# Local attention on one core: the scores of the first two query blocks joined in one matmul, and a new order of a step's pieces

## The chip, the cores and the metric

The kernel runs on one core of one Trainium2 chip. A core has a matrix engine (TensorE, PE in the profile, with its weight loads shown apart as PEld), a vector engine (VectorE, DVE), a scalar engine (ScalarE, ACT), a general engine (GpSimd, POOL) and a queue engine (SyncE, SP) that issues DMAs. Each has its own stream of instructions and works through it in order; semaphores tie the streams together. The metric is the device time of one execution in microseconds.

## The reference, cut to what matters

The whole kernel computes four residual stages on `x` of 16 sequences, 128 tokens, 128 features: causal attention, six layers of local attention with feed-forward behind a geometric warp, gated linear attention, and expert layers. The change touches the six layers of local attention alone. Each has 16 heads of 64, and queries in four blocks of 32 that see their own block and the one before:

```python
def local_attention(q, k, v):
    b, h, n, d = q.shape
    w = WINDOW                      # 32
    nw = n // w                     # 4 blocks of 32 queries
    ...
    bk2, bv2 = (look(bk), look(bv)) # keys of the block before and of the block itself
    ...
    mask = (it < jb) | (it > jb + w) | (jb == -1)
    sim = jnp.einsum('bhwie,bhwje->bhwij', bq, bk2) * QK_SCALE
    sim = jnp.where(mask, -jnp.finfo(sim.dtype).max, sim)
    attn = jax.nn.softmax(sim, -1)
    out = jnp.einsum('bhwij,bhwje->bhwie', attn, bv2)
    ...
for i in range(DEPTH):              # 6
    x = attn_layer(shift_tokens(x), Wqkv[i], q_scale[i], k_scale[i], Wo[i]) + x
    x = ffn_layer(shift_tokens(x), ln_g[i], ...) + x
```

Block 0 has no block before it. The kernel lets it look at keys 0 to 63, as block 1 does, and the mask (the tile `band`) hides the keys of block 1 from it.

## The kernel before, in words

The kernel keeps all 16 sequences on the chip. A front stage does the first attention and the warp, a local stage the six layers (96 units: one unit is one sequence in one layer), and a tail the rest. In the trace scores() of the local stage runs from 467 us to 2110 us.

A unit's work is cut into **pieces**, one method call each:

- project (four matmuls of 128x512, queries and keys), square and cossin (ACT and DVE read the result), sum_squares, lengths, rotate, normalize_queries and normalize_keys: rotary embedding and lengths, on DVE, ACT and POOL
- transpose and keep_transpose: rotated queries and keys turned to `qkT0`, `qkT1`, through TensorE (L854) and ACT
- values, keep_values, shift: values, and four DMAs on SP's queue that place the neighbour block's values in `vx`
- scores (L882), mask, maxima, exponentials, normalize: the attention weights
- turn, keep_turn, weigh (L947), keep_weighed, out, add: weights times values, and the output projection
- the feed-forward of a group of four sequences: mean, center, square, variance, root, spread (two DMAs, through memory and back), scale, up, gelu, gate, down, add

Four units go through together in a pass of `STEP`, a list of pieces written out by hand. `p0` to `p3` are the projection pieces of the four units of the pass, `t0` to `t3` the attention pieces of the units two behind, `o0` to `o3` the weighing pieces of the units three behind; `f` is the feed-forward one group behind, `e`, `g` and `h` that two groups behind. `run_layers` runs STEP once for each group of four (a shorter list FIRST for the first). The pieces issue their instructions in the list's order on TensorE, DVE, ACT and POOL under a manual schedule: each engine does its own pieces in just this order, and waits where an operand isn't there. PSUM holds two score tiles (ring `s`) and four single banks (ring `g`).

scores() of a unit makes 16 heads' scores of 128 queries by 64 keys. Heads are taken in pairs: one head's 64 features lie in partitions 0 to 63 (`LO`), the other's in 64 to 127 (`HI`). For each pair, each half and each block of 32 queries there is one matmul with 32 columns of queries as weights and 64 columns of keys moving, 64 matmuls in all. In the built program each is declared as a tile of 64 rows by 32 columns of the array, and the places (two row halves, four column groups) make eight such tiles. weigh() has 48 matmuls, all declared as 64x64 tiles; the other matmuls of a step are declared as 128x128. An fp32 matmul appears in the trace as two passes, each with a weight load.

Of the kernel before, what the change touches and what calls it, by code (L numbers as in the profile page):

```python
# [314 lines left out]
class FirstUnit:  # L315
# [19 lines left out]
    def scores(self, half):  # L335

        sc = self.sc[half] = self.fr.ps("w")
        cols = slice((self.b % 2) * P, (self.b % 2) * P + P)
        T = self.halves[half].T
        for j in range(4):  # L340
            pr = 4 * half + j
            for k, rows in enumerate((LO, HI)):
                self.nc.tensor.matmul(
                    sc[:, k * 512 + j * P : k * 512 + j * P + P],
                    T[0][rows, pr, cols], T[1][rows, pr, cols], start=True, stop=True,
                )
# [417 lines left out]
class Unit:  # L764
# [111 lines left out]
    def scores(self):  # L876
        sc = self.sc = self.lo.ps("s")
        for pr in range(8):
            for k, rows in enumerate((LO, HI)):
                for i in range(4):  # L880
                    w = 32 * max(i - 1, 0)
                    self.nc.tensor.matmul(  # L882
                        sc[32 * i : 32 * i + 32, 512 * k + 64 * pr : 512 * k + 64 * pr + 64],
                        self.T[0][rows, pr, 32 * i : 32 * i + 32],
                        self.T[1][rows, pr, w : w + 64], start=True, stop=True,
                    )

# [189 lines left out]


STEP = """
p0.project(0,0) p0.project(0,1) p0.cossin(0,0) p0.cossin(0,1) p0.square(0,0) p0.project(1,0)  # L1080
t0.transpose(1,0) p0.square(1,0) p0.square(0,1) p0.project(1,1) p0.square(1,1) t0.values(0)
t0.keep_transpose(1,0) t0.keep_values(0) p0.cossin(1,0) t0.transpose(0,0) p0.rotate(0)
p0.cossin(1,1) t0.transpose(1,1) t0.transpose(0,1) t0.keep_transpose(0,0) t0.keep_transpose(1,1)
t0.keep_transpose(0,1) p0.sum_squares(0) o0.turn(0) e.variance() o0.keep_turn(0)
t1.transpose(1,0) e.root() t0.scores() t1.transpose(1,1) t1.keep_transpose(1,0)
p0.sum_squares(1) t1.keep_transpose(1,1) o0.turn(1) t0.mask() o0.keep_turn(1) p0.lengths()
t1.transpose(0,0) t1.keep_transpose(0,0) p1.project(0,0) p0.rotate(1) p0.normalize_queries()
t1.transpose(0,1) o0.weigh() p1.square(0,0) t0.maxima() t1.keep_transpose(0,1) t1.scores()
t0.exponentials(0) p1.cossin(0,0) p1.project(0,1) o0.keep_weighed(0) p1.cossin(0,1)
p1.project(1,0) o0.keep_weighed(1) t0.values(1) p1.square(0,1) e.spread() t0.keep_values(1)  # L1090
t2.transpose(0,0) t2.keep_transpose(0,0) p1.cossin(1,0) e.scale() t1.mask() p1.square(1,0)
o0.out() o0.add() p0.normalize_keys() p1.rotate(0) t0.normalize(0) t0.exponentials(1)
p1.project(1,1) t1.values(0) t1.keep_values(0) p1.cossin(1,1) t0.shift() g.up(2) p1.square(1,1)
g.gelu(2) g.up(1) g.gelu(1) g.gate(2) t2.transpose(1,0) g.gate(1) t2.transpose(0,1)
t2.keep_transpose(1,0) t2.transpose(1,1) p1.sum_squares(0) g.up(0) t2.keep_transpose(0,1)
t2.keep_transpose(1,1) o1.turn(0) t0.normalize(1) t1.maxima() g.gelu(0) o1.turn(1) p1.rotate(1)
g.gate(0) o1.keep_turn(0) p2.project(1,0) t1.exponentials(0) t1.values(1) o1.keep_turn(1)
p2.project(0,0) h.down() p1.sum_squares(1) p2.square(1,0) t1.keep_values(1) p1.lengths()
p1.normalize_queries() p2.cossin(0,0) p2.cossin(1,0) t1.normalize(0) p1.normalize_keys()
p2.project(0,1) h.add() p2.project(1,1) p2.cossin(0,1) p2.square(0,0) o1.weigh() t2.scores()  # L1100
t1.exponentials(1) p2.square(0,1) t3.transpose(0,0) p2.cossin(1,1) o1.keep_weighed(0)
p2.square(1,1) t2.mask() t3.transpose(0,1) t1.shift() t1.normalize(1) o1.keep_weighed(1)
t2.maxima() t3.keep_transpose(0,0) t3.transpose(1,0) t3.keep_transpose(0,1) t2.values(0)
t3.keep_transpose(1,0) t2.keep_values(0) p2.rotate(0) t3.transpose(1,1) o2.turn(0)
t3.keep_transpose(1,1) o2.turn(1) o2.keep_turn(0) o2.keep_turn(1) t3.scores() p2.sum_squares(1)
t3.mask() o2.weigh() p2.rotate(1) t2.exponentials(0) o2.keep_weighed(0) t2.values(1) o1.out()
p3.project(1,0) p2.sum_squares(0) o2.keep_weighed(1) t2.normalize(0) t2.keep_values(1)
t2.exponentials(1) p3.project(0,0) t3.maxima() o1.add() p3.square(0,0) t3.values(0) p2.lengths()
p3.cossin(1,0) p3.square(1,0) o2.out() t2.normalize(1) t2.shift() p3.cossin(0,0) o3.turn(0)
t3.keep_values(0) p2.normalize_queries() o3.turn(1) o2.add() p3.project(0,1) t3.exponentials(0)  # L1110
p2.normalize_keys() o3.keep_turn(0) o3.keep_turn(1) p3.cossin(0,1) p3.project(1,1) o3.weigh()
p3.square(1,1) p3.square(0,1) f.mean() p3.cossin(1,1) p3.rotate(0) p3.sum_squares(0)
o3.keep_weighed(0) o3.keep_weighed(1) t3.exponentials(1) t3.values(1) o3.out() p3.sum_squares(1)
t3.keep_values(1) p3.rotate(1) p3.lengths() f.center() t3.normalize(0) o3.add() t3.shift()
f.square() t3.normalize(1) p3.normalize_keys() p3.normalize_queries()
""".split()


# [896 lines left out]
```

## Time and profile before

| what | value |
|---|---|
| median of 3 runs | 2503.51 us (2493.62 to 2518.77) |
| the profiled execution | 2485.3 us, its span 2483.5 us |
| granted clock of TensorE, mean | 0.975 |
| PE, DVE, ACT, POOL busy, share of the span | 91%, 73%, 68%, 60% |
| PE matmul records, weight load records | 32244, 32244 |
| scores(), L882: matmul passes, busy | 12288, 158.8 us |
| weigh(), L947: matmul passes | 9216 |
| local stage (440 to 2120 us): PE busy | 1522.1 of 1680 us |

The page of a profile describes one execution on the chip. "Busy" is the time in which at least one instruction of an engine runs; tiles of the array that work side by side count once, so 12,288 passes of 0.226 us each make 158.8 us. Records of matmuls overlap, and their ends are modelled: what tells how fast TensorE goes is the distance from start to start. Idle time is listed with what ended it; "issue" means that the engine waited for nothing that the profile shows.

### The profile page before, as it was taken

The numbers are of one execution on the slowest core, as the hardware profiler recorded it, in microseconds if no ns is written. First come the engines' busy times: TensorE is split into PE (matmuls) and PEld (weight loads), VectorE is DVE, ScalarE is ACT, GpSimd is POOL, SyncE is SP. The second block draws the span as 40 slices with busy tenths as digits, with TensorE's granted clock in tenths as the row PEclk, the third lists the DMA queues.
The fourth block names the chain that finished last, engine by engine and source line by source line (L and its number), as shares of the span: only waits on it lengthen the run. The fifth ranks groups of instructions, "written<-read, shape, count | busy, mean of one in ns | idle before, by whom it ended". The sixth has DMA issues, their size and how long they took to land. (4 is left out here: it accounts for less than half of the span.)

```text
span 2483.5 us, 77001 instructions
## 1 busy us (share of the span) xinstructions
PE 2249.8 (91%) x32244; PEld 1540.3 (62%) x32244; DVE 1803.6 (73%) x2481; ACT 1695.4 (68%) x5814; POOL 1482.2 (60%) x1242
## 2 busy tenths in 40 slices
PE   7999998789899979998989999999899999789998
PEld 5676765466556656665656666666556666456766
DVE  6999998777677777777777778777677777454545
ACT  5888888577677757777777777777677777344422
POOL 3777776676566666666666776666666665243210
PEclk9999999999999989999999999999999999899999
DMA  3111114111111111211112111211111111212220
GB/s 111 31 30 32 28 31 112 35 36 36 40 57 52 36 39 37 66 44 32 44 44 67 39 44 37 70 39 40 30 37 37 38 34 41 60 51 69 72 73 26
DMA packets 120034, 116.67 MB, mean 47 GB/s; under 512 B 62914, under 2 KB 81928, under 8 KB 118920
## 3 DMA queue, kind: packets, MB, share of 16 engines
q1 hardware_dynamic: 108712, 87.62, 13.0%
q0 software_dynamic: 9216, 22.03, 2.9%
q8 instruction: 254, 4.16, 0.7%
q10 hardware_dynamic: 1760, 2.10, 0.3%
q14 instruction: 92, 0.75, 0.1%
HBM read 54.77 MB, written 6.60 MB: 25 GB/s over the span
## 5 line engine op out<-in xcount | busy, mean ns | idle before, releaser
L820 POOL TENSOR_TENSOR rot<-t 128x512 f32<-128x512 f32 x384 | 492.7, 1312 | 120.9 <-DVE t L794 120.8
L794 DVE TENSOR_TENSOR t<-g,tab 128x1024 f32<-128x1024 f32 x372 | 449.2, 1222 | 154.5 <-PE g L781 134.2
L907 ACT ACTIVATE pe<-s,nm 128x64 f32<-128x64 f32 x1536 | 460.5, 340 | 1.3 <-DVE nm L896 1.0
L916 POOL TENSOR_TENSOR pe<-pe,den 128x512 f32<-128x512 f32 x192 | 199.7, 1046 | 391.5 <-DVE den L915 317.6
L831 POOL TENSOR_TENSOR rot<-rot,r 128x1024 f32<-128x1024 f32 x192 | 363.1, 1909 | 52.3 <-ACT r L813 52.3
L781 PE MATMUL g<-wqkv,xs 128*128 128x512 f32 x744 | 377.8, 621 | 1.7 <-ACT sq L786 1.0
L907 ACT ACTIVATION_READ_ACCUMULATOR pe<-s,nm 128x1 f32 x1536 | 357.8, 233 | 0.0
L786 ACT ACTIVATE sq<-g 128x512 f32<-128x512 f32 x372 | 220.4, 600 | 182.4 <-DVE t L794 126.9
L859 ACT COPY qkT<-g 128x512 f32<-128x512 f32 x384 | 213.5, 592 | 122.8 <-PE g L854 122.5
L854 PEld LDWEIGHTS g<-ident,rot 128*128 128x128 f32 x1536 | 180.6, 145 | 105.2 <-issue 69.8
L882 PE MATMUL s<-qkT,qkT 64*32 64x64 f32 x12288 | 158.8, 226 | 85.0 <-issue 85.0
L804 DVE TENSOR_REDUCE ss<-sq 128x16 f32<-128x1024 f32 x192 | 229.8, 1208 | 0.0
L854 PE MATMUL g<-ident,rot 128*128 128x128 f32 x1536 | 220.1, 281 | 10.7 <-ACT ge L1049 6.6
L963 PEld LDWEIGHTS g<-oT,wo 128*128 128x128 f32 x1536 | 188.5, 195 | 39.1 <-issue 24.9
L839 PE MATMUL g<-wqkv,xs 128*128 128x512 f32 x384 | 208.2, 625 | 2.3 <-ACT qkT L859 2.2
L882 PEld LDWEIGHTS s<-qkT,qkT 64*32 64x32 f32 x12288 | 133.6, 106 | 105.6 <-issue 103.7
L963 PE MATMUL g<-oT,wo 128*128 128x128 f32 x1536 | 191.8, 279 | 2.4 <-ACT oT L955 2.4
L781 PEld LDWEIGHTS g<-wqkv,xs 128*128 128x128 f32 x744 | 131.0, 196 | 100.9 <-issue 69.4
L890 DVE TENSOR_TENSOR s<-s,band 128x1024 f32<-128x1024 f32 x96 | 117.9, 1228 | 87.4 <-PE s L882 87.2
L947 PE MATMUL g<-pT,vx 64*64 64x32 f32 (+1 forms) x6144 | 161.6, 218 | 19.5 <-issue 19.4
L450 POOL DMA_INDIRECT box<-fr_image,idx x128 | 157.0, 1227 | 33.6 <-issue 30.9
L947 PE MATMUL g<-pT,v 64*64 64x64 f32 (+1 forms) x3072 | 162.7, 228 | 14.0 <-issue 13.5
(345 smaller groups left out, 4540.9 us busy)
## 6 DMA issues: line engine op xcount, KB each, us to landing
vx<-v SPq DMA_DIRECT2D x384, 128.0 KB
wqkv<-in_lo_wqkv_dram SPq DMA_DIRECT2D x6, 1536.0 KB
roots<-lo_roots SPq DMA_DIRECT2D x23, 256.0 KB
fr_image<-xres SPq DMA_DIRECT2D x32, 104.0 KB
wo<-in_lo_wo_dram SPq DMA_DIRECT2D x6, 512.0 KB
box<-fr_image,idx POOLq DMA_INDIRECT x128
fr_moved<-out SPq DMA_DIRECT2D x16, 128.0 KB
w<-in_lo_w_dram SPq DMA_DIRECT2D x6, 341.0 KB
```

Source lines behind the costliest of these rows:

```text
L781: self.nc.tensor.matmul(pq, self.xT, self.w.qkv[:, at : at + 512], start=True, stop=True)
L786: self.nc.scalar.activation(self.bank["sq", k][:, c * 512 : c * 512 + 512], self.bank["q", k, c], AF.Square)
L794: self.nc.vector.tensor_tensor(self.t[k][:, :, 8 * c : 8 * c + 8, :], heads(self.bank["q", k, c]).unsqueeze(1).to_broadcast([P, 2, 8, 64]) ...
L804: self.nc.vector.tensor_reduce(self.ss[:, 16 * k : 16 * k + 16], heads(self.bank["sq", k]), AX.X, ALU.add)
L820: self.nc.gpsimd.tensor_tensor(self.rot[k][:, :, at], t[:, 0, :, at], t[:, 1, :, other], ALU.add)
L831: self.nc.gpsimd.tensor_tensor(self.rot[k], self.rot[k], self.r[:, 16 * k : 16 * k + 16].unsqueeze(2).to_broadcast([P, 16, 64]), ALU.mult,)
L854: self.nc.tensor.transpose(pt[:, j * P : j * P + P], flat[:, at : at + P], self.s.ident)
L859: self.nc.scalar.copy(self.T[k][:, 4 * c : 4 * c + 4, :].rearrange("p c t -> p (c t)"), self.bank["T", k, c],)
L882: self.nc.tensor.matmul(sc[32 * i : 32 * i + 32, 512 * k + 64 * pr : 512 * k + 64 * pr + 64], self.T[0][rows, pr, 32 * i : 32 * i + 32], s ...
L907: self.nc.scalar.activation(self.pe[half][:, n, :], heads(self.sc)[:, at, :], AF.Exp, bias=self.nm[:, at : at + 1], accum_out=self.den[:, ...
L947: self.nc.tensor.matmul(po[half][(LO, HI)[k ^ half], j * P + q0 : j * P + q0 + n], v, self.pT[half][rows, j, q0 : q0 + n], start=True, sto ...
L963: self.nc.tensor.matmul(self.pout[:, 0:P], self.w.o[:, c, :], self.oT[:, c, :], start=(c == 0), stop=(c == 7),)
```

## The change

Two things change, both in the local stage.

First, scores() makes one matmul of queries 0 to 63 (blocks 0 and 1, which both look at keys 0 to 63) where it made two of 32; blocks 2 and 3 keep theirs. A unit has 48 score matmuls for 64. In the built program the joined one is declared as a tile of 64x64, the other two as 64x32, and they are issued in turn: 64x64, 64x32, 64x32 for LO, the same for HI, for each of eight pairs.

Second, the list STEP holds the same pieces in another order. The roles p, t, o, e, f, g and h and their distances stay.

```diff
         for pr in range(8):
             for k, rows in enumerate((LO, HI)):
-                for i in range(4):
-                    w = 32 * max(i - 1, 0)
+                for q0, n, w in ((0, 64, 0), (64, 32, 32), (96, 32, 64)):
                     self.nc.tensor.matmul(
-                        sc[32 * i : 32 * i + 32, 512 * k + 64 * pr : 512 * k + 64 * pr + 64],
-                        self.T[0][rows, pr, 32 * i : 32 * i + 32],
+                        sc[q0 : q0 + n, 512 * k + 64 * pr : 512 * k + 64 * pr + 64],
+                        self.T[0][rows, pr, q0 : q0 + n],
                         self.T[1][rows, pr, w : w + 64], start=True, stop=True,
                     )
...
 STEP = """
-p0.project(0,0) p0.project(0,1) p0.cossin(0,0) p0.cossin(0,1) p0.square(0,0) p0.project(1,0)
-t0.transpose(1,0) p0.square(1,0) p0.square(0,1) p0.project(1,1) p0.square(1,1) t0.values(0)
...
-t1.transpose(1,0) e.root() t0.scores() t1.transpose(1,1) t1.keep_transpose(1,0)
...
-t1.transpose(0,1) o0.weigh() p1.square(0,0) t0.maxima() t1.keep_transpose(0,1) t1.scores()
...
-p2.project(0,1) h.add() p2.project(1,1) p2.cossin(0,1) p2.square(0,0) o1.weigh() t2.scores()
...
-t3.keep_transpose(1,1) o2.turn(1) o2.keep_turn(0) o2.keep_turn(1) t3.scores() p2.sum_squares(1)
-t3.mask() o2.weigh() p2.rotate(1) t2.exponentials(0) o2.keep_weighed(0) t2.values(1) o1.out()
...
+t0.transpose(0,0) t0.keep_transpose(0,0) t0.transpose(1,0) p0.project(1,0) t0.keep_transpose(1,0)
+p0.cossin(1,0) p0.project(0,0) p0.square(1,0) t0.transpose(0,1) p0.cossin(0,0) p0.project(0,1)
...
+t0.scores() t1.transpose(1,0) t0.keep_values(1) t1.transpose(0,0) t1.transpose(1,1)
...
+e.root() t1.scores() p1.cossin(1,1) t0.normalize(0) e.spread() o0.turn(1) p1.square(1,1) t0.shift()
...
+p1.square(0,1) o0.weigh() t1.values(1) p1.sum_squares(1) o0.keep_weighed(0) t1.keep_values(0)
...
+o1.turn(1) p1.rotate(0) p2.cossin(0,0) p2.square(0,1) p2.square(1,0) t2.scores() t1.shift()
...
+p1.normalize_queries() o1.keep_turn(1) o0.out() p2.square(1,1) o1.keep_turn(0) e.scale() g.up(1)
...
+g.up(2) t1.normalize(1) g.gelu(0) g.gelu(2) t1.normalize(0) g.gate(0) o1.weigh() t2.maxima()
...
+o2.weigh() o2.keep_weighed(0) p3.project(0,1) p3.project(1,0) p3.cossin(0,1) t2.exponentials(1)
+t2.normalize(0) t3.scores() o2.keep_weighed(1) o1.out() p2.lengths() p3.cossin(1,0) p3.square(0,1)
...
```

## The prediction

> **What bounds the kernel now.** I read the busy shares first, then the stage that the change touches, then what TensorE's idle time ends in, then single instructions.
>
> ```profile
> span 2483.5 us, 77001 instructions
> ...
> PE 2249.8 (91%) x32244; PEld 1540.3 (62%) x32244; DVE 1803.6 (73%) x2481; ACT 1695.4 (68%) x5814; POOL 1482.2 (60%) x1242
> ...
> q8 instruction: 254, 4.16, 0.7%
> ```
>
> TensorE (PE) is busy for 91% of the span and the next engine for 73%. Queue q8 moved 4.16 MB in 254 packets, 16,384 bytes each; TensorE's 32,244 matmuls and 32,244 weight loads at 64 bytes make 4.13 MB, so this queue refills TensorE's instructions, 256 at a time. The table by stage (us, then busy time and count of PE, PEld, DVE, ACT, POOL, then clock and DMA) has this row for the six local-attention layers:
>
> ```profile
> 440.00:2120.00 1680.00, 1522.12 (x27031) 1031.65 (x27029) 1225.47 (x1544) 1216.13 (x4515) 1097.45 (x889) 0.98 0.15 43
> ```
>
> TensorE idles 158 us of 1680 there; DVE and ACT idle over 450. A pass of STEP (four units) takes 69 us, of which TensorE works 63 and DVE and ACT some 51 each. TensorE sets the end, and whatever is added to it there is paid. The waits of TensorE (idle us, times, longest):
>
> ```profile
> PE s L882 <- issue: 85.0, 58, 2.8
> PE g L947 <- issue: 33.0, 23, 2.1
> ```
>
> "issue" means that nothing the profile shows was missing. All lies in the two places where instructions are densest: scores() (L882, 64 matmuls, each of two passes with a weight load of its own: 256 instructions, one block of q8) and weigh() (L947, 192). Taken from the starts of single passes, a gap over 0.3 us counting as a stall less one normal pass, scores() loses 94.4 us in 58 of 96 units and weigh() 37.1 us in 24: **131.5 us of refill stalls**. That is nearly all of the idle time; some 27 us are left.
>
> Next, what one scores() costs and what surrounds it. Columns: start, us, engine, line, tile shape (rows*columns of the array), count.
>
> ```profile
> 1272.01 1.48 PE L882 MATMUL s<-qkT,qkT 64*32 64x64 f32 x128
> 1273.42 0.66 PE L854 MATMUL g<-ident,rot 128*128 128x128 f32 x4
> ...
> 1868.35 0.60 PE L854 MATMUL g<-ident,rot 128*128 128x128 f32 x4
> 1868.79 1.04 PE L923 MATMUL g<-ident,pe 128*128 128x128 f32 x8
> 1869.75 0.45 PE L882 MATMUL s<-qkT,qkT 64*32 64x64 f32 x32
> ```
>
> A scores() without a stall takes 1.41 us from its first start to the next line's (1273.42 - 1272.01). Within it the 128 passes span 1.266 us, 10 ns a pass, because eight tiles of 64x32 (two row halves by four column groups) work side by side. Now the seams. Four passes of L854 and then L923, both 128*128, are 0.44 us apart, 0.109 each. Eight passes of L923 and then L882, of another shape, are 0.96 us apart: 8 x 0.109 = 0.87, and **0.09 for the change of shape**. The single records give the same at each seam: 0.109 from a 128-wide pass to the next of its shape and 0.202 to another shape; 0.429 and 0.522 for a 512-wide one; from L882 (64x32) to L947 (64x64) 0.145, from L947 to L882 0.149. Less the streaming of 64 columns (0.053, from 0.429 x 64/512), that is again 0.09. A changed column count of the weights inside a declared 128x128 tile (L1040, 85 to 128) stays at 0.429: it is the declared tile shape that costs.
>
> After a seam the first weight load isn't ahead. In weigh():
>
> ```profile
> 1276.18 0.27 PE L947 MATMUL g<-pT,v 64*64 64x64 f32 x1
> 1276.18 0.27 PE L947 MATMUL g<-pT,vx 64*64 64x64 f32 x1
> 1276.19 0.27 PE L947 MATMUL g<-pT,v 64*64 64x64 f32 x1
> 1276.20 0.27 PE L947 MATMUL g<-pT,vx 64*64 64x64 f32 x1
> 1276.28 0.22 PE L947 MATMUL g<-pT,v 64*64 64x64 f32 x1
> ```
>
> The first passes of four tiles start 7 ns apart and last 0.27 instead of 0.22; the second pass of the first tile starts 0.107 later (median of all entries) instead of 0.053. Entering scores() that figure is 0.080. So each entry pays a weight load (0.053 for 64 columns, 0.027 for 32) and then a pass.
>
> **The change, part by part.**
>
> *Joined scores.* Per unit 48 matmuls instead of 64: 96 x 16 = 1536 fewer, 6144 fewer instructions, 24 refills of 254. But the joined matmul has 64 weight columns and is declared as a 64x64 tile, the other two stay 64x32, and the loop issues 64x64, 64x32, 64x32 for each of 8 pairs and 2 halves. Counted over the built programs, neighbours of different shape go from 599 to 3643; 31 a unit are inside scores(). One of the 16 groups then costs:
> - 64x64: first to second pass 0.107, then to the next shape 0.146: 0.253.
> - 64x32, two tiles at once: the second tile's second pass starts 0.080 + 0.007 after the first, then 0.146: 0.233.
> - Sum 0.486; 16 groups 7.78, less the last seam, which was there before: 7.63 us from first to last start, against 1.27. **+6.36 us a unit, x 96 = +611 us.**
>
> No row shows shapes alternating this quickly, so both ends: if the seam's 0.146 swallowed everything else, 16 x 2 x 0.146 - 0.15 = 4.5 us (+310); if weights load ahead of the seam, 16 x (0.053 + 0.146 + 0.060 + 0.146) - 0.15 = 6.3 us (+486). I take 7.63, because all 96 entries into scores() and 97 into weigh() show the late load. [...] Read as waiting until the last matmul has ended, 0.216 us by the records, the group would be 0.107 + 0.216 + 0.087 + 0.216 = 0.63 and the sum (10.0 - 1.27) x 96 = +838. [...]
>
> *Refill stalls.* In scores() 192 instructions now take 7.6 us, 40 ns each, in place of 256 in 1.4. Only weigh() stays dense (192 in 1.4 us), and its block holds at least 64 others, of 40 ns or more: some 4 us a block, against the at most 2.8 + 1.4 us that the longest stall shows for a refill behind a dense block. So most stalls go: between -80 and -131, I take **-112 us**. [...] The row says 256 instructions in 1.41 us, 5.5 ns each, and 131 us of waits exactly there, so I follow the row.
>
> *The order.* The same pieces in a new sequence on every engine. The 68 further seams cost 68 x 0.093 = +6 us. Table loads on ACT fall from 70 to 68 (2 x 1.28 us, hidden: ACT has 18 us to spare in a pass). Moved pieces with DMAs are shift() (four on SP's queue) and spread() (two, the second behind the first). spread() still stands ahead of t0.shift(), with e.scale() now much later, so the round trip has more cover; every shift() stands well ahead of the weigh() of its unit (t0.shift() of o1.weigh(), and so on to t3.shift(), which serves the next pass), and no DMA stands among TensorE's waits for L947 today. SP moves nothing on the path. The waits of ACT on DVE (L786 133 us), of DVE on PE (L794 134 us) and of POOL on DVE (L916 318 us) will change places, but TensorE's pass grows from 63 to 63 + 4 x 6.4 = 89 us against 51 for DVE and ACT and 46 for POOL, so they are covered by 38 us a pass. Of the 27 us of other idle time I count nothing; a bad order could add as much again. The granted clock of 0.98 could gain or lose: fewer long stalls, but an array that is drained half of the time in scores().
>
> **Sum** on the profiled execution: 2485.3 + 611 - 112 + 6 = 2990. Its own time lies 0.7% below the median of the runs, 2503.5; with the same +505 the median would be 3008. I forecast between the two, **3000 us**, a little under 20% slower. TensorE's 20 us more a pass times 24 passes gives the same size.
>
> **The rivals.**
> - *Seams are cheap when shapes alternate (ends on the other side).* Mechanism: tiles of both shapes lie in different column groups, and the array might overlap them, so that the seams seen today are paid only where all columns are shared. Then scores() is issue-bound: 96 passes x 10 ns = 0.95 us, -30 us, and the stalls go: 2503.5 - 30 - 112 = **2360**. It decides where scores() with its stalls costs less than today's, that is under 1.27 + 112/96 = 2.4 us, a seam under some 0.04 us. For it: different tiles do overlap within one shape. Against: the last tile of scores() (L882) and the first of weigh() (L947) share no row and no column of the array, and the seam between them costs its 0.145 all the same. Chance 0.08.
> - *Weights load ahead, or a seam absorbs the pass:* 2503.5 + 486 - 112 + 6 = **2884**, down to 2708. For it: within one shape loads run ahead. Chance 0.20.
> - *Full drain, or the clock halves in the drained stretches:* 2503.5 + 838 - 112 + 6 = **3235**. For it: the clock's record has windows of 3.4 us at half speed in this stage, one of them right after the 2.9 us stall at 1278 us. Chance 0.08.
> - *The order wins or loses by itself and the seams don't matter:* within 1%, 0.02.
> - My forecast, 2900 to 3130: 0.62.
>
> About 1% is what a measurement of this kernel can tell from no change (runs spread over 2494 to 2519). Slower 0.90, same 0.02, faster 0.08. The range 2750 to 3120 takes in the forecast and most of the weights-ahead case.
>
> **What would show it.** Right: the group of 64*64 and 64*32 passes of scores() spread over 7 to 8 us a unit, starts of neighbouring shapes 0.146 apart, TensorE idle on "issue" at scores() near zero and at weigh() below 30 us, a STEP pass of 85 to 92 us, and DVE, ACT and POOL with lower shares. Wrong: scores() under 2.4 us, or a pass near 69 us, or new waits of TensorE for ACT or DVE of more than 100 us. If scores() comes out at 4.5 to 6.4 us, the seam is right and the late weight load wrong.

## The result, and the profile after

The changed kernel takes **3282.6 us** (median; 3282.3 to 3288.3) against 2498.7 us: 1.315 times the time before, 95% interval 1.310 to 1.320. The forecast had the sign and the place right and the size wrong: 3000 us was said, with 3120 as the upper end.

The page of the changed kernel, the lines that answer to those shown of before:

```profile
span 3280.5 us, 70978 instructions
...
PE 3180.9 (97%) x29172; PEld 2115.1 (64%) x29172; DVE 1796.3 (55%) x2481; ACT 1694.9 (52%) x5812; POOL 1467.5 (45%) x1242
...
PEclk9999988788787788788887887878878788778999
...
q8 instruction: 230, 3.77, 0.5%
```

TensorE is now busy for 97% of the span, with 3072 matmul records and 24 packets of q8 fewer: 6144 instructions, 256 for each packet. DVE and ACT do what they did before, in a longer span. New is the clock row: 7 and 8 tenths from one end of the local stage to the other. Before, it was 9 in all slices but two:

```profile
PEclk9999999999999989999999999999999999899999
```

The row of the stage after the change says the same (mean clock third from the right):

```profile
440.00:2900.00 2460.00, 2434.30 (x23753) 1594.00 (x23751) 1213.01 (x1535) 1213.57 (x4508) 1082.17 (x890) 0.82 0.11 29
```

0.82 where it was 0.98, and an idle time of 26 us where it was 158. Of TensorE's waits on issue, only this one is left among the longer ones, and it lies at 458 us, ahead of the first scores():

```profile
PE w L753 <- issue: 3.5, 1, 3.5
```

One scores() (now L881) in the timeline of TensorE:

```profile
1544.49 1.02 PE L839 MATMUL g<-wqkv,xs 128*128 128x512 f32 x2
1545.44 9.46 PE L881 MATMUL s<-qkT,qkT 64*64 64x64 f32 x96
1554.84 1.54 PE L854 MATMUL g<-ident,rot 128*128 128x128 f32 x6
```

It takes 9.40 us to the next line's start; before it was 1.41. And two windows of 4 us inside this same piece (PE busy and count, PEld, DVE, ACT, POOL, then the clock):

```profile
1545.40:1549.40 4.00, 4.00 (x50) 2.69 (x50) 1.61 (x2) 1.34 (x3) 4.00 (x5) 1.00 0.66 198
1550.40:1554.40 4.00, 4.00 (x32) 2.52 (x32) 0.00 (x0) 0.00 (x0) 0.00 (x0) 0.50 0.00 0
```

TensorE counts as busy throughout both windows. In the first the clock is full and 50 passes start, in the second it is half and 32 do. The clock's record of this unit: it falls at 1550.3 us, 4.9 us after scores() began, and stays at half for 10.2 us, beyond the end of scores().

**Where the 796 us of the stage went.** From the starts of single records between the first and the last pass of scores(), gaps over 0.3 us counted as idle; "half" is the part of it at half clock (us):

| kernel | scores() | half | weigh() | other matmuls | half | idle | sum |
|---|---|---|---|---|---|---|---|
| before | 152 | 4 | 155 | 1191 | 62 | 145 | 1643 |
| changed | 926 | 504 | 143 | 1351 | 395 | 19 | 2439 |
| order_alone (below) | 137 | 0 | 143 | 1179 | 15 | 35 | 1493 |

scores() gained 774 us, the other matmuls 160, and idle time and weigh() lost 138. At full clock a group of scores() (one 64x64 matmul, two of 64x32) takes 0.488 us from first start to first start, at half clock 0.753 (medians of groups that lie wholly in one state).

### The profile page after: what moved, and what is told of

Its sections match the earlier page's. It is cut to its first block, busy times and chain, and to the rows that moved or that the text cites. A ratio compares the mean times of both kernels' runs of the same rounds, so it can differ in the third digit from the quotient of the medians.

```text
span 3280.5 us, 70978 instructions
## 1 busy us (share of the span) xinstructions
PE 3180.9 (97%) x29172; PEld 2115.1 (64%) x29172; DVE 1796.3 (55%) x2481; ACT 1694.9 (52%) x5812; POOL 1467.5 (45%) x1242
## 3 DMA queue, kind: packets, MB, share of 16 engines
q1 hardware_dynamic: 108712, 87.62, 10.2%
## 4 chain that ended last, share of the span: by engine, by line
PE 91%; DVE 4%; issue 2%; ACT 1%; POOL 1%; DMA 1%; DVEq 0%; POOLq 0%; SPq 0%; ACTq 0%
PE s L881 28%; PE g L781 12%; PE g L962 7%; PE g L854 6%; PE g L839 6%; PE g L946 4%; PE g L1039 4%; PE g L922 3%; PE w L510 3%; PE g L292 2%; PE g L1064 2%; PE e L1573 1%; DVE diag L463 1%; PE o L1591 1%; PE e L1741 1%
## 5 line engine op out<-in xcount | busy, mean ns | idle before, releaser
L881 PE MATMUL s<-qkT,qkT 64*32 64x64 f32 (+1 forms) x9216 | 933.0, 271 | 0.0
L881 PEld LDWEIGHTS s<-qkT,qkT 64*32 64x32 f32 (+1 forms) x9216 | 594.0, 132 | 374.6 <-issue 160.9
L781 PE MATMUL g<-wqkv,xs 128*128 128x512 f32 x744 | 427.2, 685 | 0.0
L928 DVE COPY pT<-g 128x512 f32<-128x512 f32 x192 | 128.0, 688 | 486.5 <-PE g L922 485.8
L906 ACT ACTIVATION_READ_ACCUMULATOR pe<-s,nm 128x1 f32 x1536 | 343.9, 224 | 0.0
L962 PEld LDWEIGHTS g<-oT,wo 128*128 128x128 f32 x1536 | 246.6, 250 | 41.5 <-issue 33.2
L854 PEld LDWEIGHTS g<-ident,rot 128*128 128x128 f32 x1536 | 213.8, 163 | 70.6 <-issue 50.7
L962 PE MATMUL g<-oT,wo 128*128 128x128 f32 x1536 | 248.5, 334 | 2.4 <-ACT oT L954 2.4
L854 PE MATMUL g<-ident,rot 128*128 128x128 f32 x1536 | 238.9, 311 | 1.6 <-ACT qkT L859 1.2
L839 PE MATMUL g<-wqkv,xs 128*128 128x512 f32 x384 | 218.8, 653 | 1.6 <-ACT qkT L859 1.5
L946 PEld LDWEIGHTS g<-pT,v 64*64 64x64 f32 x3072 | 130.8, 135 | 82.1 <-issue 33.9
```

What stands on the lines that cost most here:

```text
L781: self.nc.tensor.matmul(pq, self.xT, self.w.qkv[:, at : at + 512], start=True, stop=True)
L839: self.nc.tensor.matmul(pv, self.xT, self.w.qkv[:, 2048 + c * 512 : 2560 + c * 512], start=True, stop=True)
L854: self.nc.tensor.transpose(pt[:, j * P : j * P + P], flat[:, at : at + P], self.s.ident)
L881: self.nc.tensor.matmul(sc[q0 : q0 + n, 512 * k + 64 * pr : 512 * k + 64 * pr + 64], self.T[0][rows, pr, q0 : q0 + n], self.T[1][rows, pr, ...
L906: self.nc.scalar.activation(self.pe[half][:, n, :], heads(self.sc)[:, at, :], AF.Exp, bias=self.nm[:, at : at + 1], accum_out=self.den[:, ...
L946: self.nc.tensor.matmul(po[half][(LO, HI)[k ^ half], j * P + q0 : j * P + q0 + n], v, self.pT[half][rows, j, q0 : q0 + n], start=True, sto ...
```

## The experiments

Unless said otherwise an edit is made in the changed kernel. My theory after the result: the seams between tile shapes cost what was forecast, and they also bring the clock to half, which was not. Two rivals: the joined 64-column tile is slow by itself, or the new order is what costs. For the "some 3 us" of the theory below, the trace of the changed kernel has 2.7 to 6.1 us from the start of a scores() to the fall of the clock; that TensorE is drained in that time, no record shows.

**order_alone**: the new STEP with the scores() of before.

```diff
-                for q0, n, w in ((0, 64, 0), (64, 32, 32), (96, 32, 64)):
+                for i in range(4):
+                    w = 32 * max(i - 1, 0)
...
```

> The new order of STEP with the scores() of before (64 matmuls of one tile shape). Seams-and-clock theory (each neighbour of another tile shape costs 0.093 us and a late weight load, and a TensorE that is drained for some 3 us falls to half clock): scores() stays at 1.27 us a unit, the clock at 0.97, and the time at 2400 to 2510 us, depending on how many of the 131 us of refill stalls this order still has. Rival, the joined 64-column tile is slow by itself: the same. Rival, the order is what costs: above 3000 us.

Measured: 2339.2 us, 0.936 of before (0.933 to 0.939). The order is no cost but a gain of 161 us, more than was expected. scores() stays at 1.285 us a unit. In its waits of TensorE (idle us, times, longest) nothing of L882 and L947 is among the longer ones; the first line of the local stage is a wait for L1034, and L882 stands far down:

```profile
PE w L510 <- DVE diag L463: 18.4, 15, 5.7
PE g L1040 <- DVE xn L1034: 9.6, 21, 0.8
...
PE s L882 <- issue: 1.0, 2, 0.7
```

So this order has no refill stalls to speak of, with scores() as dense as before.

**joined_alone**: the joined scores() in the old STEP.

```diff
-                for i in range(4):
-                    w = 32 * max(i - 1, 0)
+                for q0, n, w in ((0, 64, 0), (64, 32, 32), (96, 32, 64)):
...
```

> The joined scores() in the old order. Seams-and-clock theory: scores() at 9 to 10 us a unit, clock 0.85, 3250 to 3320 us. Rival, the joined tile is slow by itself: the same. Rival, the order is what costs: 2400 to 2500 us.

Measured: 3311.0 us, 1.324 of before (1.319 to 1.328). The whole loss comes with the joined scores() (906.5 us from first to last starts, 903.2 in the changed kernel). The gain of the order shrinks to 28 us, because a scores() of 9 us leaves no stalls to remove: idle time falls to 32 us in the old order too.

**by_shape**: the same 48 matmuls, all of one shape ahead of the other.

```diff
-        for pr in range(8):
-            for k, rows in enumerate((LO, HI)):
-                for q0, n, w in ((0, 64, 0), (64, 32, 32), (96, 32, 64)):
+        for part in (((0, 64, 0),), ((64, 32, 32), (96, 32, 64))):
+            for pr in range(8):
+                for k, rows in enumerate((LO, HI)):
+                    for q0, n, w in part:
...
```

> The changed kernel, with the same 48 matmuls a unit issued shape by shape: sixteen of 64x64 first, then thirty-two of 64x32, so one seam inside scores() in place of 31. Seams-and-clock theory: 32 passes on two tiles at 0.058 us make 0.93 us, a seam 0.15, 64 passes on four tiles 0.9 to 1.3, so 2.0 to 2.4 us a unit, the clock back near 0.97, stalls below 40 us: 2440 to 2510 us. Rival, the joined tile is slow by itself: most of the loss stays, above 3000 us.

Measured: 2387.2 us, 0.954 of before (0.951 to 0.957). scores() takes 1.960 us in each of 96 units, a little under the estimate, and none of it at half clock. The same matmuls in another sequence are 895 us faster: it is the alternation, and the rival that the joined tile is slow by itself falls. But joining isn't a gain either: 48 us slower than order_alone, with a longer scores() (1.96 us for 1.285) in which two and then four tiles take turns instead of eight.

**by_pair**: two halves together, 15 seams inside scores() for 31.

```diff
-            for k, rows in enumerate((LO, HI)):
-                for q0, n, w in ((0, 64, 0), (64, 32, 32), (96, 32, 64)):
+            for part in (((0, 64, 0),), ((64, 32, 32), (96, 32, 64))):
+                for k, rows in enumerate((LO, HI)):
+                    for q0, n, w in part:
...
```

> The changed kernel, with the two halves of a pair of heads brought together by shape: two 64x64, then four 64x32, so 15 seams inside scores(). Seams-and-clock theory: 8 x (0.107 + 0.007 + 0.146 + 0.080 + 0.020 + 0.146) less 0.15 is 3.9 us a unit at full clock: +253 us, -131 us of stalls, 2620 us; if the clock falls in part, up to 2800. Rival, the joined tile is slow by itself: as the changed kernel, about 3280 us.

Measured: 2582.4 us, 1.033 of before (1.030 to 1.037). scores() takes 3.914 us, as worked out (3.9), and no part of it is at half clock. (2620 was too high because it started from before with its stalls taken off, not from 2339.) With 1, 15 and 31 seams scores() takes 1.96, 3.91 and 7.66 us at full clock (16 x 0.488 less the last seam). That isn't one price a seam: the first 14 further seams add 0.14 us each, the next 16 add 0.23; I put that down to tiles of one shape that no longer start side by side. The sum by parts, seam and late weight load (an estimate from the distances of starts in before), gives both.

**one_shape**: joined matmuls for both halves of the queries. The last block's scores against its own keys are left out.

```diff
-                for q0, n, w in ((0, 64, 0), (64, 32, 32), (96, 32, 64)):
+                for q0, n, w in ((0, 64, 0), (64, 64, 32)):
```

> The changed kernel with joined matmuls for both halves of the queries, all of 64x64 (32 a unit); the scores of the last block against its own keys are left out and those it gets are of other keys. No seam inside scores(). Seams theory: 64 passes on four tiles, 16 x 0.055 + 0.05 = 0.93 us a unit, against 1.28 with the old scores() in this order: 2339 - 33 = 2306 us, 2290 to 2330. Rival, the 64-column tile is slow by itself: above 2600 us.

Measured: 2311.3 us, 0.921 of before (0.917 to 0.926). scores() takes 0.943 us. Joining without a change of shape is a gain, of 28 us against order_alone, though this kernel doesn't compute the reference.

These runs leave the clock. What brings it down: the seams, the length of the stretch, or too little work in it?

**in_parts**: scores() in four parts with 128-wide pieces between.

```diff
-    def scores(self):
-        sc = self.sc = self.lo.ps("s")
-        for pr in range(8):
+    def scores(self, part):
+        if part == 0:
+            self.sc = self.lo.ps("s")
+        sc = self.sc
+        for pr in (2 * part, 2 * part + 1):
...
-t2.scores() t1.shift() ... o1.turn(0) p2.project(1,1) ... o0.out() ... g.up(1) ... t2.mask()
+t2.scores(0) t1.shift() ... p2.project(1,1) t2.scores(1) ... o0.out() t2.scores(2) ... g.up(1) t2.scores(3) ... t2.mask()
```

> The changed kernel with scores() issued in four parts of two head pairs (1.95 us each at full clock), and 0.9 to 1.8 us of 128-wide pieces between the parts; mask() of t0 and t3 stands later for it. The seams are all there, but no stretch of alternating tiles lasts over 2 us. If the half clock comes from long stretches: scores() at 7.6 us a unit at full clock, half-clock time under 100 us, and the changed kernel's 3283 less the 168 us inside scores() and the some 150 us behind it, plus 30 for new seams: 2960 to 3020 us. Rival, the half clock comes with the load as a whole or with each seam: 3250 to 3330 us.

Measured: 3152.3 us, 1.257 of before (1.251 to 1.262), between the two expectations. The clock did come back: half-clock time in the stage falls from 904 to 232 us, in scores() from 504 to 30, and scores() with its new seams takes 761 us for 926. Against that, TensorE's idle time rises from 19 to 102 us, most of it in a wait that the edit made:

```profile
PE g L781 <- DVE xs L972: 73.3, 23, 3.2
```

The wait is for an output addition on DVE, which stands in DVE's order behind t3.mask(), which now waits for the last part; I read it that the addition frees the PSUM bank that project() is to have. The other matmuls, 1291 us, still have 163 us at half clock. So the half clock can be taken from scores() by breaking it up, with the seams all there, but this edit gave a good part of it back.

**by_pair_twice**: by_pair with each scores() issued twice over.

```diff
-        for pr in range(8):
+        for pr in list(range(8)) * 2:
```

> by_pair with its 48 score matmuls issued twice, the second over the first (the same numbers): 8.0 us of two and four tiles at a time, 31 seams. Rival A, length decides: a stretch of 8 us halves the clock as it did in the changed kernel, scores() above 9 us, 3200 to 3300 us. Rival B, how much of the array works decides: 8.0 us at full clock, 2582 + 96 x 4.05 = 2970 us.

Measured: 2960.2 us, 1.180 of before (1.174 to 1.186), rival B to within 10 us. A window of 4 us inside it:

```profile
1300.00:1304.00 4.00, 4.00 (x104) 2.75 (x96) 0.43 (x1) 1.60 (x5) 0.78 (x2) 1.00 0.01 4
```

Full clock (of the 770 us of scores(), 11 are at half), and 104 passes where the changed kernel starts 50. The run has as many seams as the changed kernel, twice its score matmuls, and a longer scores() at full clock (8.0 us against 7.66), and is **322 us faster**. So neither the number of seams nor the length alone brings the clock down.

**by_tile**: order_alone with the score matmuls sorted by tile.

```diff
-        for pr in range(8):
-            for k, rows in enumerate((LO, HI)):
-                for i in range(4):
-                    w = 32 * max(i - 1, 0)
+        for k, rows in enumerate((LO, HI)):
+            for i in range(4):
+                w = 32 * max(i - 1, 0)
+                for pr in range(8):
...
```

> The new order with the scores() of before, its 64 matmuls of one shape sorted so that the eight of one tile follow one another: no seam, but one tile (an eighth of the array) at a time, unless the queue lets the next tile begin. Serial: 128 passes x 0.053 = 6.8 us a unit, 2339 + 530 = 2870 us at full clock; if little use of the array is enough to halve the clock, 3050 to 3250 us. If the queue overlaps tiles: 3 to 4 us, 2500 to 2600 us.

Measured: 2740.7 us, 1.093 of before (1.087 to 1.098). scores() takes 5.762 us, 45 ns a pass: little overlap from tile to tile, and full clock throughout, with 14.8% of the array at work and a tile streaming for 97% of the time (both estimates from the starts, as in the last table).

**filled**: the second matmul of a group made 64 columns wide, the third written over its last rows.

```diff
-                for q0, n, w in ((0, 64, 0), (64, 32, 32), (96, 32, 64)):
+                for q0, n, w in ((0, 64, 0), (64, 64, 32), (96, 32, 64)):
```

> The changed kernel with the second matmul of each group made 64 columns wide (queries 64 to 127 against keys 32 to 95; the third then writes over the rows of the last block): as many matmuls, instructions and seams, in the same alternation, but two quarters of the array in the 64x64 phase and one eighth in the other. A group takes 0.107 + 0.007 + 0.146 + 0.080 + 0.146 = 0.486 us at full clock, the same as in the changed kernel. Tiles in use, weighted by streaming time: 4 x 1/4 x 0.053 + 2 x 1/8 x 0.053 over 0.486 = 13.6% of the array, against 10.9% in the changed kernel (half clock) and 14.4% in by_tile (full clock). Rival A, the share of the array that works decides, with a bound below 13.6%: full clock, scores() at 7.7 us, 2339 + 96 x 6.4 = 2950 us. Rival B, the rate of passes or the number of seams decides (as in the changed kernel): half clock, 3260 to 3300 us, or the bound lies between 13.6 and 14.4%.

Measured: 3287.0 us, 1.313 of before (1.307 to 1.318): rival B. With 14.2% of the array at work for 11.1% (estimates, as in the last table) it is the changed kernel again, scores() from first to last starts 903.1 us for 903.2, of it at half clock 480.3 us for 480.7. The groups by shape of filled, of by_pair and of by_tile, in this order (busy us, mean ns of a pass), show the shapes and counts that the edits ask for, and longer passes on the mean in filled, where half clock is part of them:

```profile
L881 PE MATMUL s<-qkT,qkT 64*64 64x64 f32 x6144 | 602.6, 282 | 0.0
L881 PE MATMUL s<-qkT,qkT 64*32 64x64 f32 x3072 | 538.7, 265 | 0.0
```

```profile
L882 PE MATMUL s<-qkT,qkT 64*64 64x64 f32 x3072 | 254.5, 243 | 0.0
L882 PE MATMUL s<-qkT,qkT 64*32 64x64 f32 x6144 | 242.7, 228 | 0.0
```

```profile
L882 PE MATMUL s<-qkT,qkT 64*32 64x64 f32 x12288 | 573.9, 218 | 0.0
```

Last, where the order's own gain of 161 us comes from.

**dense_neighbours**: order_alone with three scores() moved next to a weigh().

```diff
-... t1.scores() p1.cossin(1,1) ... o0.weigh() ...
+... p1.cossin(1,1) ... t1.scores() o0.weigh() ...
-... t2.scores() t1.shift() ... t2.mask() g.gelu(1) ... o1.weigh() t2.maxima()
+... t1.shift() ... g.gelu(1) ... t2.scores() o1.weigh() t2.mask() t2.maxima()
-o2.weigh() o2.keep_weighed(0) ... t3.scores() ...
+o2.weigh() t3.scores() o2.keep_weighed(0) ...
```

> order_alone (new order, old scores()) with scores() of three of four units moved next to a weigh(): t1.scores() and t2.scores() right before o0.weigh() and o1.weigh(), t3.scores() right after o2.weigh(), mask() of t2 behind o1.weigh(). 448 instructions then issue in some 2.7 us. If the old order's stalls came from dense pieces standing together: TensorE idle on issue at scores() and weigh() comes back with 50 to 110 us, 2400 to 2460 us. Rival, the gain of the order lies elsewhere: 2335 to 2350 us.

Measured: 2540.5 us, 1.012 of before (1.009 to 1.015): the stalls are back, and it loses more than they are.

```profile
PE g L947 <- issue: 71.0, 35, 4.0
PE s L882 <- issue: 25.2, 20, 2.0
PE g L1040 <- DVE xn L1034: 20.4, 24, 1.3
```

96 us on issue where order_alone had 1, and 11 more on L1034. The rest of the 201 us is in the other matmuls (1242 us for 1179, with 91 us at half clock for 15) and in weigh(), 16 us. The sites of the stalls are shown; how much of the rest follows from them and how much from the moved pieces was not separated.

**by_shape_old_order**: by_shape's scores() in the old STEP (the diff of by_shape).

> The old order with the 48 joined matmuls a unit issued shape by shape (1.96 us a unit, 192 instructions, 10 ns each). Refill theory: scores() now issues little more slowly than a refill takes, so part of the 131 us of stalls goes: 2500 + 96 x 0.68 = 2565 less 60 to 120, 2445 to 2505 us. Rival, the order alone removes stalls, whatever scores() is: 2565 us.

Measured: 2428.7 us, 0.968 of before (0.965 to 0.971), under the expected 2445. With a scores() that issues 10 ns an instruction in place of 5 there are fewer stalls:

```profile
PE s L882 <- issue: 24.2, 29, 3.6
...
PE g L947 <- issue: 7.7, 12, 1.3
```

32 us are left of 118 in this view. Joining by shape costs 60 us in scores() and takes away more than that in stalls, in this order; in the new one, which has none, it only costs. The fastest kernel of the study that computes the reference is **order_alone, 2339 us**.

## Why the prediction was right or wrong

- *TensorE sets the end.* Right: DVE, ACT and POOL did the same work in a longer span, and what was added to TensorE was paid: 796 us in the stage, 797 in the span.
- *Joined scores, +611 us.* Right at full clock: 0.146 and 0.148 for the two seams and 0.107 for the second pass at 64x64 stand in the records, a group takes 0.488 us for 0.486 forecast, so 7.66 us a unit, and 16 x 0.488 x 96 is 613 us above order_alone's 137. The late weight load, which was taken from entries into weigh() and scores() alone, holds in all 821 groups that lie wholly at full clock, the last of a unit left out (0.106 to 0.108 after a seam into 64x64, 0.080 into 64x32). That each change of shape costs time is borne out. No run shows the full drain of a rival, a wait at each seam for the recorded end of the last matmul (0.216 us a seam, +838): 0.146 was measured.
- *Refill stalls, -112 us.* Right, somewhat low: all 131 us went. The trace of before bears out that they are refills: of its 82 gaps of starts over 0.3 us in scores() and weigh(), 74 end 1.2 to 1.6 us after a packet of q8 has landed, and the other 8 are under 1 us. But the part that the text gives to slow scores() would have gone by the order alone, as order_alone shows.
- *The order, +6 us.* Wrong in size and sign. It was costed by its seams, and its waits were counted as covered; what it does is keep the dense pieces apart, so that it alone saves 161 us by the medians and 150 in the stage of the profiled executions. By the single gaps 131 us of stalls went; in the table they stand as 110 us of idle time and as part of the 27 in scores() and weigh(). Another 12 went in the other matmuls, of which 15 us run at half clock for 62. In the changed kernel this is hidden: joined_alone shows only 28 us of it left.
- *The clock: the step that failed.* The forecast set "the granted clock of 0.98 could gain or lose" at nothing, and named halving only in a rival of chance 0.08, whose 3235 us was worked out from a full drain (+838) with no term for the clock. The text's "drained half of the time" is in no record; by the estimate below a tile streams for 47% of the time. That 3235 lies near the result is luck: the seam stayed at 0.146 us, and the clock made up the difference. It halves within 95 of the 96 scores(), 2.7 to 6.1 us after the start, and stays down for 6.8 or 10.2 us (93 of 98 times in the stage). Order_alone's 2339 and 613 for the seams make 2952; the other **331 us** are the clock's: 926 - 137 - 613 = 176 in scores() and 1351 - 1179 = 172 in what comes behind it (395 us at half clock for 15), less 16 us of other idle time that is covered now. The half-clock record of scores() alone gives the same: 504 us with groups of 0.753 for 0.488 us have lost 177.
- *The clock fell without a gap.* In the trace of before each of the 20 half-clock stretches of the stage begins 1.3 to 4.5 us after the start of an idle time of TensorE of over 1 us; one of 2.78 us at 1278.45 us is followed by half clock from 1281.92 to 1285.33 us. In the changed kernel TensorE had no gap: the profile shows it busy for 4.00 of 4.00 us at half clock, and all through the 3.4 us ahead of each of the 95 falls in scores().
- *What it counts instead: open.* As an estimate, let a pass stream for 0.429 us at 512 columns, the distance of starts in before, and for 0.053 at 64, in proportion. The parts of scores() at full clock then have these medians ("values moved in": columns times the rows of the tile, of 128):

| kernel | clock | columns, summed over tiles | values moved in | share of the array | time in which any tile streams |
|---|---|---|---|---|---|
| changed | halves | 66% | 33% | 11.1% | 47% |
| filled | halves | 67% | 34% | 14.2% | 47% |
| by_tile | full | 118% | 59% | 14.8% | 97% |
| by_pair and by_pair_twice | full | 127% | 64% | 21% | 53% |

Each of the four parts the halving kernels from the others, the share of the array only just. The whole stage of all thirteen traces says more. Cut on the clock's own changes into windows of 3.413 us (18 of the 20 half-clock stretches in before last one of them, the 6.8 and 10.2 us of the changed kernel two and three), it has 6270 windows at full clock, and 408 of them are followed by half clock. With the bound that suits each measure best, values moved in (38%) put 40 windows on the wrong side, the time in which any tile streams (47.5%) 62, the share of the array (14.4%) 118 and summed columns (66%) 170. The bounds are fitted to these windows, so this ranks the measures and proves none: the sum of columns is the weakest, and between the first two no run decides. The number of passes a microsecond is excluded: a 512-column matmul starts 2.3 and keeps the clock, the changed kernel 12.

## What to carry to other kernels

Count the declared tile shape from one matmul to the next before joining or splitting small matmuls: here a change costs 0.09 us plus a weight load of 0.03 to 0.05 (estimates from the distances of starts), and 31 of them a unit cost 943 us with the clock, where joining without them saved 28 (one_shape, which leaves out scores that the reference needs). Then ask what the stretch does to TensorE's clock: "busy" in the records did not keep it up here (4.00 of 4.00 us at half clock), so work out for what share of the time a tile really streams (47% lost the clock here, 53% kept it; that this is what counts is not shown), and read the clock row before anything else of a profile after. And where an engine idles on issue, put the pieces with the most instructions per microsecond apart before making them fewer (1 us of stalls in order_alone, 96 in dense_neighbours).

## What the runs showed of the hardware that was not expected

- TensorE's clock halves without any gap in its records: in 95 of 96 scores(), where by the estimate above a tile streams for 47% of the time, and in none of by_pair at 53% and by_tile at 97%; it comes back 6.8 or 10.2 us later, so that 395 us of other matmuls ran at half clock too.
- Refills of TensorE's instructions need not show even where 256 instructions issue in 1.4 us: 1 us of stalls in order_alone, 96 us when the same pieces stand next to others as dense.
- By the start times, weight loads don't run ahead across a change of tile shape in any of the 821 groups at full clock; tiles of one shape that stand one after the other overlap only a little (by_tile, 45 ns a pass, where 53 is the estimate for one alone).
